# Graph network on one core: a pool that outlives the statistics, x's sums by order edges, and edge pieces that run into the second head

## The chip, the cores and the metric

The kernel runs on one core of a Trainium2 chip. The metric is the device time in microseconds (us) of one execution; three runs of the kernel before gave 1992.88, 1995.93 and 1997.72, so the median is 1995.93 us. The profile is that of one further execution, with a span of 1996.9 us. Engines are named as in the profile: PE does matmuls (PEld loads their weights), DVE is the vector engine, ACT the scalar engine, POOL is GpSimd, and SP holds the sync queue, which only issues transfers (SPq).

## The reference

Four layers run on one graph of N = 2708 nodes with F = 256 features and a dense float32 adjacency matrix `adj`. Each layer's result is added to x and normalised over the features.

```python
x = _layernorm(x + adj @ (x * W0))                     # layer 0
x = _layernorm(x + layernormed_attention(x, adj))      # layer 1, four heads
x = _layernorm(x + layer2(x, adj, adj))                # layer 2, below
x = _layernorm(x + layer3(x, adj))                     # cat(x, adj @ (x @ Wn.T) / (degree + 1)) @ Wl.T

def _gat_head(h, node_adj, edge_adj, W, a):            # layer 2, one of K = 3 heads
    hW = h @ W
    hp = (node_adj > 0) @ hW
    hm = (node_adj < 0) @ hW
    e_plus = leaky_relu(concat([hp, hm]) @ a)[:, 0]
    e_minus = leaky_relu(concat([hm, hp]) @ a)[:, 0]
    att = where(edge_adj > 0, e_plus[None, :], NEG_INF)
    att = where(edge_adj < 0, e_minus[None, :], att)
    return softmax(att, axis=1) * edge_adj @ hW

# layer 2: adj0 is adj with a zero diagonal, d its diagonal
edge_output = gru(adj0 @ h, h, edge weights)
edge_support = mean over k of _gat_head(h, adj0, adj0, gat_W[k], gat_a[k])
node_output = gru(edge_support, h, node weights)
return d * edge_output + d * node_output
```

With the inputs of this kernel no element of `adj` is negative; a separate branch, not taken here, would deal with negative ones.

## The kernel before

Rows are handled as NT = 22 tiles of P = 128 rows (the last has 20). The adjacency is read in float32, transposed in advance (`adj_t`), and every float32 matmul appears in the profile as two passes. Layers 0 and 1 run first and end near 690 us. The change concerns what follows.

**Statistics (`e_work`, lines 801 to 887).** For each of 22 rows of tiles `row_stats` (L831) needs, per head k, the maximum and the sum of exponentials over all columns. DVE makes `none` (L846), a bfloat16 row that is NEG_INF where there is no edge. Then, three times, DVE adds it to the logits `e_b` and reduces (L850), ACT takes the exponential and its sum (L855), DVE inverts the sum (L858). The rows of `adj` are loaded by gpsimd into two places, `row2` and `arow`. At the same time PE computes `adj0 @ x` for six groups of columns (`edge_sums`, L249, matmuls at L262, blocks loaded at L191 by the sync queue) and the edge GRU of the first four groups (`gru_t`, L738). The last two groups of columns (`left`, 384 and 276 wide) keep their sums in DRAM for later. Results of the statistics are transposed and stored in DRAM by `store_stats` (L781): PE transposes, ACT copies to a row tile `sr` (L790), gpsimd stores it (L796). Nine tiles, those that the first unit needs, are stored inside this stage; the other 13 tiles form four runs for later (`other_stats`, L1165).

**Attention (L1180 to L1215).** The columns are cut into two halves of NH = 1354, and each half into three units of 512, 512 and 330. Per unit u and head k a loop runs over c = 0 to 10: a step takes tiles c and c + 11 of one half together with both halves of the columns, a block of 1 MB at full width. `load_blocks` (L934) loads it and POOL zeroes the diagonal pieces (L950). The blocks go round through three places: two buffers of "blk" in the left pool, and the tail of `turn` for every third. ACT makes p from the statistics row `st_k` (L1193, L1196), DVE multiplies p by the block (L1197), and `step` (L974) forms four sums on DVE (L980 to L983) and seven matmuls (L993), which is a product of 2x2 blocks with seven instead of eight multiplications. The other operands of it are x itself and four sums per c of x's quarters, `xq[c]`, made by `quarter_sums` (L958; four DVE operations each) in the first head of the first unit and kept. The seven accumulators fill seven of PSUM's eight banks. At the end of a head `sums` (L997) copies m1 to "m1s" on ACT (L1001) and combines the accumulators on DVE (L1004 to L1011); L1213 multiplies by the inverse sums.

**Small pieces between matmuls.** PE's last PSUM bank, `bank`, serves work that is cut into pieces by Python generators. `step` calls `between()` (L1173) after its third and its sixth matmul, two slots in a step, and each slot runs one piece: first from `urgent` (the projection of the head before, L1029, four pieces), then from `later` (the edge cells of the two left groups, L1156, 16 pieces; `other_stats`, four pieces; node cells of the unit before). In the first head `later` is filled after c = 1 with edge cells and then the statistics, and at c = 10 a loop empties it before the head's sums:

```python
if u == 0 and k == 0 and c == MH - 1:
    while later:
        between()
    node_w = load_weights()
```

`sr` of `other_stats` and `m1s` of `sums` share the tag "m1s", which has one buffer.

**Layer 3 (L1240 to L1262)** uses the same `step` and `sums` on layer 2's result, with blocks loaded straight into p (`load_pairs`, L915), three units, no heads.

**What sets the order.** The kernel is written through a framework that orders each engine's instructions at compile time, by program order and a model of when inputs are ready; an instruction later in the text may so come earlier in its engine's queue. A pool of buffers lies on a stack from the left or the right end of SBUF; a pool opened after another was closed takes over its memory, and each buffer waits for the last users of the buffers that it covers. `n_left` and `n_right` of the attention take over memory of the statistics' pools. [...]

Of the kernel before, what the change touches and what calls it, by code (L numbers as in the profile page):

```python
# [19 lines left out]
P = 128  # L20
# [7 lines left out]
def kernel(  # L28
# [770 lines left out]
    for s in (fall_stack, mask_stack, m_stack, ps_t_stack):  # L799
        s.close()  # L800
    with pool("e_work") as ework:
        with (
# [28 lines left out]
            def row_stats(i):  # L831
# [12 lines left out]
                nc.vector.tensor_tensor(blk, blk, offdiag[:n, :n], ALU.mult)  # L844
                none = rows.tile([P, N], BF16, tag="none", name="none", bufs=2)
                nc.vector.tensor_scalar(none[:n], a[:n], 0.0, NEG_INF, ALU.is_equal, ALU.mult)  # L846
# [46 lines left out]
    with (  # L893
# [5 lines left out]
        ps_a = ps_stack.enter_context(pool("ps_a", 1, space=PSUM))  # L899
        node_w = lwn = None  # L900
        loaded = 0

        def bank():
            return banks.tile([P, W], F32, tag="bank", name="bank")

        def load_stats(u, k, i):

            w = units[u][1]
            dst = nleft.tile([P, 2, W], F32, tag=f"st{i}", name=f"st{i}", bufs=2 - i)
            d = st_d[u][i * K + k]  # L910
            src = bass.AP(tensor=d.tensor, offset=d.offset, ap=[[0, P], [W, 2], [1, w]])
            nc.sync.dma_start(dst[:, :, :w], src)
            return dst
# [20 lines left out]
        def load_blocks(u, c):  # L934
# [3 lines left out]
            if loaded % 3 == 2:  # L938

                s = turn[:, NT * F - 4 * w :].rearrange("p (m h w) -> p m h w", m=2, h=2)  # L940
            else:
                s = nleft.tile([P, 2, 2, W], F32, tag="blk", name="blk", bufs=2)
            loaded += 1
# [53 lines left out]
        def sums(m, w):  # L997

            m1, m26, m75, m43 = m
            m1s = nleft.tile([P, W], F32, tag="m1s", name="m1s")  # L1000
            nc.scalar.copy(m1s[:, :w], m1[:, :w])  # L1001
# [8 lines left out]
            nc.vector.tensor_tensor(yq[:, 3], yq[:, 1], m75[:, 1, :w], ALU.add)  # L1010
            nc.vector.tensor_tensor(yq[:, 1:3], yq[:, 1:3], m43[:, :, :w], ALU.add)  # L1011
            return y

        def load_weights():
            wih, whh = weights(nleft, "wih", n_wih, nc.gpsimd), weights(nleft, "whh", n_whh, nc.gpsimd)
            nonlocal lwn
            lwn = load_lwn(nleft)
            wk = nleft.tile([P, K, FC, F], F32, name="wk")
            for k in range(K):
                nc.sync.dma_start(wk[:, k], gat_w[k].rearrange("(c p) j -> p c j", p=P))  # L1020
            return wih, whh, wk

        def project(k, y, est, w):

            for h in range(2):
                for j in range(FC):
                    pw = bank()
                    for f in range(FC):
                        nc.tensor.matmul(  # L1029
                            pw[:, :w], node_w[2][:, k, f, j * P : (j + 1) * P], y[:, f, h, :w],  # L1030
                            start=(f == 0), stop=(f == FC - 1),
                        )
# [98 lines left out]
        def node(u, est):  # L1131
# [3 lines left out]
            for h in range(2):  # L1135
                lo = h * NH + a
                xt, et = nxt or load_cell(lo, w)
                yt = nleft.tile([P, FC, W], F32, tag="yt", name="yt")
                yield from cell(est[h], xt, yt, w, *node_w[:2], b_node)
                nc.vector.tensor_tensor(yt[:, :, :w], yt[:, :, :w], et[:, :, :w], ALU.add)  # L1140
# [15 lines left out]
        def edge_cells():  # L1156
            wih, whh = weights(nleft, "wih", e_wih), weights(nleft, "whh", e_whh)
            for g in left:
# [3 lines left out]
                yield from cell(sup, xt, yt, w, wih, whh, b_edge)  # L1162
                nc.gpsimd.dma_start(edge_d[g][:, :, :w], yt[:, :, :w])

        def other_stats():  # L1165
            for run in runs(order[first:]):
                store_stats(bank(), nleft.tile([P, W], F32, tag="m1s", name="sr")[: 2 * K], *run)
                yield
# [11 lines left out]
        for u, (_, w) in enumerate(units):  # L1180
            est = [nleft.tile([P, FC, W], F32, tag="est", name="est", bufs=3) for h in range(2)]
            for k in range(K):
                m = accumulators()
                for c in range(MH):
                    if u == 0 and k == 0:
                        xq.append(quarter_sums(xs, c))
                    blk = load_blocks(u, c)
                    pa = nright.tile([P, 2, 2, W], F32, tag="p", name="p", bufs=3)
                    for i in range(2):
# [6 lines left out]
                        nc.scalar.activation(p[:, :, :w], p[:, :, :w], AF.Exp, scale=-1.0)  # L1196
                        nc.vector.tensor_tensor(p[:, :, :w], p[:, :, :w], blk[:, i, :, :w], ALU.mult)  # L1197
# [44 lines left out]
        for u, (_, w) in enumerate(units):  # L1242
            m = accumulators()
            for i, c in enumerate(lead):
# [8 lines left out]
                if i == MH - 3:  # L1253
                    o8 = nleft.tile([P, 2 * W * 4 // F // 2, F], F32, tag="blk", name="o8", bufs=2)
                    for j, t in enumerate(complete(u)):
                        nc.gpsimd.dma_start(o8[: sz(t), j], y3_d[t])
                step(m, pa, h3, hq[c], c, w, i == 0, i == MH - 1, range(7) if early3 else (2, 5))
            later.append(rows3(u, sums(m, w), o8))
        ps_stack.close()
        banks = ps_stack.enter_context(pool("ps_end", 8, space=PSUM))  # L1260
        while urgent or later:
            between()  # L1262


# [260 lines left out]
```

## Time and profile before

| stretch (us) | what runs | PE busy (us) | DVE busy | ACT busy | PE clock | DMA GB/s |
|---|---|---|---|---|---|---|
| 0 to 257 | layer 0 | 247.53 | 101.47 | 25.85 | 1.00 | 165 |
| 257 to 660 | layer 1 | 386.38 | 346.25 | 175.09 | 0.97, 0.99 | 135, 78 |
| 701 to 800 | statistics | 98.35 | 97.41 | 73.01 | 1.00 | 220 |
| 800 to 900 | statistics | 98.00 | 99.93 | 76.24 | 0.98 | 221 |
| 900 to 970 | end of the statistics | 68.90 | 66.52 | 52.05 | 1.00 | 123 |
| 984 to 1076 | first head of the attention | 92.00 | 66.80 | 54.02 | 0.98 | 205 |
| 1262 to 1467 | second unit | 202.93 | 148.04 | 109.84 | 1.00 | 139 |
| 1745 to 1816 | layer 3, first unit | 70.72 | 32.52 | 12.74 | 1.00 | 104 |

The columns give the time in which an engine executes within the stretch, the share of full speed that the throttle granted to PE, and what the transfers moved. A stretch in which PE is busy throughout is bound by PE; where it is not, the chain of waits tells what it waited for. Intervals between the rows are taken up in the prediction. Two groups of the page matter besides: L850, the reduction of the statistics on DVE, with 66 instructions of 2986 ns (196.8 us), and L993, the attention's and layer 3's matmuls, with 528 + 528 + 396 instructions in its three largest groups (643.2 us).

### The profile page before, as it was taken

Reading aid. Unit: us, or ns where it says so; the run is one execution under the profiler, and the core shown is the slowest. Engines: PE = TensorE matmul, PEld = TensorE weight load, DVE = VectorE, ACT = ScalarE, POOL = GpSimd, SP = SyncE. Lnnn points to the kernel's source line nnn. Section 1 sums busy time; section 2 is a strip of 40 time slices with the busy share of each in tenths; the row PEclk is TensorE's granted clock in tenths of the full one; section 3 lists DMA queues with packets and bytes.
Section 4 is the critical chain, followed back from the end, with each engine's and each line's share of the span. In section 5 each row is a group of like instructions: output and inputs, shape, how many; then the busy total and the mean of one; then the engine's idle time right before and its main releaser. Section 6 shows DMA issues by size and latency. Waiting matters only on the chain.

```text
span 1996.9 us, 21045 instructions
## 1 busy us (share of the span) xinstructions
PE 1898.2 (95%) x7028; PEld 948.3 (47%) x7028; DVE 1455.5 (73%) x2364; ACT 852.7 (43%) x1011; POOL 354.3 (18%) x522
## 2 busy tenths in 40 slices
PE   8999999999999999999797999999999999999995
PEld 7888822222333444445453444444444555554453
DVE  4343378898897699999866688686787668745664
ACT  0100144455604277777654556455555555311000
POOL 0211210014414301120302000121110101311211
PEclk9999999999999999999898999999999999999997
DMA  8344333433101766664665466454555444643753
GB/s 283 120 166 140 135 112 131 148 112 122 41 4 50 237 222 217 231 221 144 195 201 175 121 185 173 122 159 125 150 150 131 109 118 122 173 113 86 206 156 82
DMA packets 398211, 293.96 MB, mean 147 GB/s; under 512 B 105355, under 2 KB 379435, under 8 KB 390245
## 3 DMA queue, kind: packets, MB, share of 16 engines
q1 hardware_dynamic: 381180, 237.86, 40.6%
q0 software_dynamic: 10848, 50.23, 7.2%
q10 hardware_dynamic: 6064, 4.42, 0.7%
q8 instruction: 58, 0.95, 0.2%
q14 instruction: 61, 0.49, 0.1%
HBM read 280.03 MB, written 12.40 MB: 146 GB/s over the span
## 4 chain that ended last, share of the span: by engine, by line
PE 67%; DVE 12%; DMA 8%; ACT 4%; issue 3%; POOL 3%; SPq 1%; ACTq 0%; POOLq 0%; DVEq 0%
PE m L993 30%; PE acc L199 9%; PE bank L1053 6%; PE acc L650 5%; DMA turn<-in_adj_dram 4%; DVE z L850 4%; PE s L262 4%; PE bank L1029 3%; PE den L659 3%; ACT turn L597 2%; PE bank L1104 2%; ACT turn L599 2%; DMA blk<-in_adj_t_dram 1%; DVE p L668 1%; POOL bn_rs L151 1%
## 5 line engine op out<-in xcount | busy, mean ns | idle before, releaser
L668 DVE SCALAR_TENSOR_TENSOR p<-fall_b,rise,mask 128x1024 f32<-128x1024 f32 (+1 forms) x264 | 298.7, 1153 | 39.6 <-PE den L659 23.0
L1193 ACT ACTIVATE p<-st,e_neg 128x1024 f32<-128x1024 f32 (+1 forms) x198 | 197.3, 1040 | 192.7 <-PE m L993 185.9
L993 PE MATMUL m<-p,xq 128*128 128x512 f32 (+1 forms) x528 | 245.7, 547 | 0.0
L650 PE MATMUL acc<-p,h 128*64 128x512 f32 (+2 forms) x1056 | 227.5, 559 | 5.9 <-ACT sum L682 2.7
L993 PE MATMUL m<-s,xq 128*128 128x512 f32 (+1 forms) x528 | 226.3, 545 | 0.0
L850 DVE CUSTOM_DVE_ANT_0 z<-e_b,none 128x2708 f32<-128x2708 f32 (+1 forms) x66 | 196.8, 2986 | 0.3 <-DVE e_b L820 0.2
L855 ACT ACTIVATE z<-z,st 128x2708 f32<-128x2708 f32 (+1 forms) x66 | 168.6, 2554 | 62.1 <-DVE st L850 60.2
L993 PE MATMUL m<-p,x 128*128 128x512 f32 (+1 forms) x396 | 171.2, 552 | 19.3 <-DVE p L1197 13.8
L199 PE MATMUL acc<-turn,strip 128*128 128x256 f32 (+1 forms) x836 | 187.1, 379 | 0.0
L1196 ACT ACTIVATE p<-p 128x1024 f32<-128x1024 f32 (+1 forms) x198 | 179.3, 943 | 0.3
L980 DVE TENSOR_TENSOR s<-p 128x512 f32<-128x512 f32 (+1 forms) x132 | 82.7, 627 | 125.5 <-PE m L993 106.6
L262 PE MATMUL s<-blk,x 128*128 128x512 f32 (+2 forms) x416 | 164.9, 550 | 0.7 <-ACT supt L269 0.7
L1197 DVE TENSOR_TENSOR p<-p,blk 128x1024 f32<-128x1024 f32 (+1 forms) x132 | 143.6, 1104 | 29.3 <-ACT p L1196 15.4
L199 PEld LDWEIGHTS acc<-turn,strip 128*128 128x128 f32 (+1 forms) x836 | 151.9, 185 | 23.5 <-issue 0.2
L993 PEld LDWEIGHTS m<-p,xq 128*128 128x128 f32 x528 | 99.7, 191 | 98.1 <-issue 74.4
L993 PEld LDWEIGHTS m<-s,xq 128*128 128x128 f32 x528 | 99.3, 191 | 93.6 <-issue 70.6
L650 PEld LDWEIGHTS acc<-p,h 128*64 128x64 f32 x1056 | 65.0, 137 | 150.7 <-issue 118.5
L659 PE MATMUL den<-p,h 128*32 128x512 f32 (+2 forms) x1056 | 125.9, 558 | 2.3 <-DVE p L668 1.9
L151 POOL TENSOR_TENSOR bn_rs<-bn_rs,neg_half 128x1 f32<-128x1 f32 (+1 forms) x110 | 78.4, 713 | 242.6 <-DVE bn_rs L150 239.7
L993 PEld LDWEIGHTS m<-p,x 128*128 128x128 f32 x396 | 75.3, 192 | 93.4 <-issue 59.3
L262 PEld LDWEIGHTS s<-blk,x 128*128 128x128 f32 x416 | 78.8, 193 | 76.2 <-issue 62.8
L950 POOL TENSOR_TENSOR blk<-blk,offdiag 128x128 f32<-128x128 f32 (+3 forms) x50 | 53.1, 1065 | 344.8 <-DMA blk<-in_adj_t_dram 296.7
(228 smaller groups left out, 2556.6 us busy)
## 6 DMA issues: line engine op xcount, KB each, us to landing
blk<-in_adj_t_dram SPq DMA_DIRECT2D x172, 256.0 KB, 3.5
turn<-in_adj_dram SPq DMA_DIRECT2D x22, 1354.0 KB, 5.9
strip<-in_adj_t_dram SPq DMA_DIRECT2D x19, 1408.0 KB, 6.4
blk<-in_adj_t_dram SPq DMA_DIRECT2D x88, 192.0 KB, 4.0
turn<-in_adj_t_dram SPq DMA_DIRECT2D x65, 256.0 KB, 3.8
arow<-in_adj_dram POOLq DMA_DIRECT2D x10, 1354.0 KB, 6.8
turn<-in_adj_dram POOLq DMA_DIRECT2D x10, 1354.0 KB, 7.0
blk<-in_adj_t_dram SPq DMA_DIRECT2D x103, 128.0 KB, 2.6
```

What stands on the lines that cost most here:

```text
L199: nc.tensor.matmul(acc, s[:, c, :n], rhs(c), start=(c == 0), stop=(c == NT - 1))
L262: nc.tensor.matmul(acc[f][:, :w], xs[c][:, f * P : (f + 1) * P], s[:, c - c0, :w], start=(c == 0), stop=(c == NT - 1),)
L650: nc.tensor.matmul(acc[s][i * HD : (i + 1) * HD, :ws], hs[c][:, 2 * q + i, :HD], ps[i][:, p0 : p0 + ws], **flags,)
L659: nc.tensor.matmul(den[j : j + CT, :ws], hs[c][:, 2 * q + i, HD + 1 - CT :], ps[i][:, p0 : p0 + ws], **flags,)
L668: nc.vector.scalar_tensor_tensor(p[:, :w], falls[g // 2][:, 2 * q + i, :w], rise[:, c, 2 * q + i : 2 * q + i + 1], mask[:, c, at : at + w] ...
L850: nc.vector.tensor_tensor_reduce(out=z[:n], in0=e_b[:n, k, :], in1=none[:n], scale=-1.0, scalar=HIGHEST, op0=ALU.add, op1=ALU.min, accum_o ...
L855: nc.scalar.activation(z[:n], z[:n], AF.Exp, scale=-1.0, bias=st[:n, t, 0, k : k + 1], accum_out=den[:n])
L993: nc.tensor.matmul(dst[:, :w], lt, rt, start=start, stop=stop)
L1053: nc.tensor.matmul(g[:, :w], lt, rt, start=(q == 0), stop=(q == len(terms) - 1))
L1193: nc.scalar.activation(p[:, :, :w], st_k[:, :, :w], AF.Relu, scale=-1.0, bias=e_neg[:, at, k : k + 1])
L1196: nc.scalar.activation(p[:, :, :w], p[:, :, :w], AF.Exp, scale=-1.0)
L1197: nc.vector.tensor_tensor(p[:, :, :w], p[:, :, :w], blk[:, i, :, :w], ALU.mult)
```

## The change

It has five parts. A pool `hold` on the right side is opened before the statistics and closed at the very end; the first buffers of the logits row "st0", one of the three places of the blocks (and of layer 3's `o8`) move there from the left pool, so that they need not wait for memory of the statistics. To make room, `none` has one buffer in place of two. The sums of x's quarters are no longer all free to run ahead: two are made at the start, and those for c + 2 are ordered on DVE after the product of step c. The first head's pieces are not forced out at its end: the statistics come first, the edge cells run on into the second head, the head's projection has its own weights `head_w` (loaded, with `lwn`, after c = 1), the node weights are loaded after the last edge cell, and "m1s" has two buffers. In layer 3 every DVE instruction traced inside a step is ordered after the last of the `sums` before it.

`issue_after(i)` adds no wait of its own: it only puts the instructions of the block behind `i` in the queue of `i`'s engine.

```diff
+    hold_stack = ExitStack()
+    hold = hold_stack.enter_context(pool("hold", side="right"))
     with pool("e_work") as ework:
...
-                none = rows.tile([P, N], BF16, tag="none", name="none", bufs=2)
+                none = rows.tile([P, N], BF16, tag="none", name="none")
...
-            dst = nleft.tile([P, 2, W], F32, tag=f"st{i}", name=f"st{i}", bufs=2 - i)
+            dst = (nleft if i else hold).tile([P, 2, W], F32, tag=f"st{i}", name=f"st{i}", bufs=2 - i)
...
-                s = nleft.tile([P, 2, 2, W], F32, tag="blk", name="blk", bufs=2)
+                s = (nleft if loaded % 3 else hold).tile([P, 2, 2, W], F32, tag="blk", name="blk")
...
-            m1s = nleft.tile([P, W], F32, tag="m1s", name="m1s")
+            m1s = nleft.tile([P, W], F32, tag="m1s", name="m1s", bufs=2)
...
-            nc.vector.tensor_tensor(yq[:, 1:3], yq[:, 1:3], m43[:, :, :w], ALU.add)
+            nonlocal summed
+            summed = nc.vector.tensor_tensor(yq[:, 1:3], yq[:, 1:3], m43[:, :, :w], ALU.add)
...
         def load_weights():
-            wih, whh = weights(nleft, "wih", n_wih, nc.gpsimd), weights(nleft, "whh", n_whh, nc.gpsimd)
             nonlocal lwn
...
         def edge_cells():
...
+            nonlocal node_w
+            node_w = weights(nleft, "wih", n_wih, nc.gpsimd), weights(nleft, "whh", n_whh, nc.gpsimd)
...
-                    if u == 0 and k == 0:
-                        xq.append(quarter_sums(xs, c))
+                    if u == 0 and k == 0 and c == 0:
+                        xq += [quarter_sums(xs, 0), quarter_sums(xs, 1)]
...
-                        nc.vector.tensor_tensor(p[:, :, :w], p[:, :, :w], blk[:, i, :, :w], ALU.mult)
+                        made = nc.vector.tensor_tensor(p[:, :, :w], p[:, :, :w], blk[:, i, :, :w], ALU.mult)
+                    if u == 0 and k == 0 and c + 2 < MH:
+
+                        with tc.issue_after(made.ins):
+                            xq.append(quarter_sums(xs, c + 2))
                     step(m, pa, xs, xq[c], c, w, c == 0, c == MH - 1, (2, 5))
                     if u == 0 and k == 0 and c == 1:
-                        later += [edge_cells(), other_stats()]
-                    if u == 0 and k == 0 and c == MH - 1:
-                        while later:
-                            between()
-                        node_w = load_weights()
+                        later += [other_stats(), edge_cells()]
+                        head_w = load_weights()
...
-                step(m, pa, h3, hq[c], c, w, i == 0, i == MH - 1, range(7) if early3 else (2, 5))
+                with tc.issue_after(summed.ins):
+                    step(m, pa, h3, hq[c], c, w, i == 0, i == MH - 1, range(7) if early3 else (2, 5))
```

More of the change, by code (lines that the diff above doesn't have):

```diff
@@ L899 @@
         ps_a = ps_stack.enter_context(pool("ps_a", 1, space=PSUM))
-        node_w = lwn = None
+        node_w = head_w = lwn = None
+        summed = None
         loaded = 0
@@ L1020, in load_weights @@
                 nc.sync.dma_start(wk[:, k], gat_w[k].rearrange("(c p) j -> p c j", p=P))
-            return wih, whh, wk
+            return wk
         def project(k, y, est, w):
@@ L1029, in project @@
                         nc.tensor.matmul(
-                            pw[:, :w], node_w[2][:, k, f, j * P : (j + 1) * P], y[:, f, h, :w],
+                            pw[:, :w], head_w[:, k, f, j * P : (j + 1) * P], y[:, f, h, :w],
                             start=(f == 0), stop=(f == FC - 1),
@@ L1138, in node @@
                 yt = nleft.tile([P, FC, W], F32, tag="yt", name="yt")
-                yield from cell(est[h], xt, yt, w, *node_w[:2], b_node)
+                yield from cell(est[h], xt, yt, w, *node_w, b_node)
                 nc.vector.tensor_tensor(yt[:, :, :w], yt[:, :, :w], et[:, :, :w], ALU.add)
@@ L1163, in edge_cells @@
                 nc.gpsimd.dma_start(edge_d[g][:, :, :w], yt[:, :, :w])
+            nonlocal node_w
+            node_w = weights(nleft, "wih", n_wih, nc.gpsimd), weights(nleft, "whh", n_whh, nc.gpsimd)
         def other_stats():
             for run in runs(order[first:]):
-                store_stats(bank(), nleft.tile([P, W], F32, tag="m1s", name="sr")[: 2 * K], *run)
+                store_stats(bank(), nleft.tile([P, W], F32, tag="m1s", name="sr", bufs=2)[: 2 * K], *run)
                 yield
@@ L1253 @@
                 if i == MH - 3:
-                    o8 = nleft.tile([P, 2 * W * 4 // F // 2, F], F32, tag="blk", name="o8", bufs=2)
+                    o8 = (nleft if u % 2 else hold).tile([P, 4 * W // F, F], F32, tag="blk", name="o8")
                     for j, t in enumerate(complete(u)):
                         nc.gpsimd.dma_start(o8[: sz(t), j], y3_d[t])
-                step(m, pa, h3, hq[c], c, w, i == 0, i == MH - 1, range(7) if early3 else (2, 5))
+                with tc.issue_after(summed.ins):
+                    step(m, pa, h3, hq[c], c, w, i == 0, i == MH - 1, range(7) if early3 else (2, 5))
             later.append(rows3(u, sums(m, w), o8))
@@ L1262 @@
             between()
+    hold_stack.close()
     def layer3():
```

## The prediction

> **What bounds the kernel now.** I began with the page's first part: PE is busy for 1898.2 us of 1996.9, so about 99 us without a matmul are all that a change of order can win, plus what a slow clock costs after such gaps. Busy times by stretch show where the large gaps lie. The columns are PE, PEld, DVE, ACT and POOL busy, then the granted clock, DMA share and GB/s.
>
> ```profile
> PE 1898.2 (95%) x7028; PEld 948.3 (47%) x7028; DVE 1455.5 (73%) x2364; ACT 852.7 (43%) x1011; POOL 354.3 (18%) x522
> ...
> 970.00:984.00 14.00, 0.57 (x1) 0.50 (x2) 9.00 (x36) 8.60 (x10) 7.52 (x5) 0.65 1.01 280
> 1076.00:1095.00 19.00, 5.61 (x20) 2.34 (x19) 8.09 (x10) 6.68 (x9) 4.80 (x8) 0.70 0.74 224
> 1095.00:1116.00 21.00, 21.00 (x43) 8.68 (x42) 11.05 (x12) 7.53 (x9) 0.00 (x0) 0.87 0.23 72
> 1116.00:1262.00 146.00, 146.00 (x339) 63.63 (x338) 126.06 (x152) 92.30 (x93) 13.31 (x15) 1.00 0.60 168
> ```
>
> PE stands for 13.4 us at 970 to 984 and again at 1076 to 1095 (19.00 - 5.61), each time followed by a slow clock. In 1116:1262, which holds two more ends of heads, it never stands: there PE is the bound, and an end of a head is free. The chain of waits says who ends each gap (start, us, what).
>
> ```profile
> 969.73 0.37 SPq L931
> ...
> 970.21 0.44 SPq L912
> ...
> 970.70 6.08 DMA blk<-in_adj_t_dram
> ...
> 976.94 5.00 POOL blk L950
> ...
> 981.96 1.43 DVE p L1197
> ...
> 983.43 17.30 PE m L993 x34
> ```
>
> At 970 the statistics end, and only then does the sync queue issue the first logits row (L912) and the first block: load, zeroed diagonal on POOL, product on DVE, first matmul.
>
> ```profile
> 1077.04 4.12 DMA st<-sr
> ...
> 1083.14 5.30 issue
> 1088.45 2.98 DMA st<-sr
> ...
> 1092.20 1.58 DMA st<-sr
> ...
> 1093.86 0.59 ACT m1s L1001
> ...
> 1094.50 6.67 PE m L993 x8
> ```
>
> At 1076 four stores of statistics pass one after the other through one buffer, "m1s", and m1 of the head's own sums must wait for the same buffer. The eight matmul passes at 1094.50 take 6.67 us; at full clock eight take 3.43.
>
> **What the Trainium skill says.** "TensorE: Matmul & The Clock Gate", section "What's actually happening": the array falls to half its clock after an idle window and needs some microseconds of activity to come back. The trace agrees: 0.65 and 0.70 in the gaps, passes of 0.83 us (6.67 / 8) for 0.43. "SBUF — State Buffer", section "Who interferes with whom": a DVE instruction with two inputs in SBUF contends with a GpSimd instruction that reads SBUF. It agrees too: a POOL L950 of 128x128 takes 4.99 us at 976.94, amid the stream of x's sums, and 0.45 at 973.08, when DVE is idle.
>
> **The change, part by part.**
>
> (1) Start of the attention. The row st0 and block c=0 go to a pool that shares no memory with the statistics' buffers, so their loads can be issued before 970 (the sync queue waits 65.4 us on PE L262 before this point, so it has room). DMA and POOL leave the path. What remains for c=0: "p" is still in memory that the statistics use, so ACT begins after its last exp at 966.46 and runs L1193 and L1196 twice (2.19 + 1.99 = 4.2): 970.7, or 971.4 with the two copies of supt (0.39 each) between. DVE's first product is then ready at about 969.8, the second at 972.6. PE ends its own L262 at 969.66, so it starts c=0 near 970 and, with the four s operations (0.6 each), ends it near 978.2. Block c=1 stays in the left pool and is now first in the queue at 970.1; c=0's landed 6.08 us after its first issue, so 976.2; POOL takes 0.5 to 5 us, one product 1.2. c=1's first matmul comes at 978 to 983; I take 980, since DVE no longer streams sums past POOL. Before, it came at 991.74. Gain 11.5 us, 8.7 to 13.7, slow clock included.
>
> (2) Pacing of x's sums. The work is unchanged (44 operations of 0.2 us issue, 8.8 us), 8 first and 4 after each product. A step of DVE then costs 2 x 1.15 + 4 x 0.6 + 4 x 0.2 = 5.5 us, below PE's 14 x 0.43 = 6.0. I cost it at nothing; PE's matmuls hide it. Queued behind the new order edge are only sums two steps ahead.
>
> (3) "none" with one buffer. Writer and reader are both DVE, in order, and from 870 to 960 each L846 already follows the third L850 of the row before (877.32 after 874.36). Only row 1's, at 695.16, ran ahead in a wait of DVE; it moves into the busy stretch: 1.56 us later for DVE and ACT at 966. This delays c=0, but c=1's block, landing at 976, sets PE's pace: nothing.
>
> (4) First head. Statistics come first, in the four slots of c=2 and 3; 14 of 16 pieces of the edge cells follow by c=10, and 2 pass into the second head behind the projection. With two "m1s" a store of 4.1 us has two slots (7 us) before its buffer is wanted. The forced end goes: 13.4 us idle and 21 x (1 - 0.87) = 2.7 of slow clock, 16.1. The matmuls moved cost PE the same elsewhere. Earlier wk and lwn (1.3 MB) compete with blocks near 990; from 970 to 1002 some 8 MB are wanted, 250 GB/s, where 280 to 345 were moved at 970 to 990: hidden, at most 3 us. The node weights wait on gpsimd for the last edge matmul, long before the first node cell.
>
> (5) Layer 3's order edge: sums before the steps of the next unit. At its entry this helps:
>
> ```profile
> 1734.23 0.69 DVE L980 TENSOR_TENSOR s<-p 128x512 f32<-128x512 f32 x1 [7.52 <-DMA p<-in_adj_t_dram]
> ...
> 1736.17 0.83 DVE L1004 TENSOR_TENSOR yk<-m1s,m 128x660 f32<-128x660 f32 x1
> ...
> 1737.06 2.08 PE L993 MATMUL m<-p,turn 128*128 128x512 f32 x2 [4.70 <-DVE yk L1004]
> ```
>
> DVE's s of the next step waits 7.52 us for a load, and the sums L1004, ready at about 1731.6, stand behind it, and PE behind them. With sums first PE waits for the load alone (to 1735.5): 1.5 to 2.5 us, I take 2. At the two later ends of units it costs: there the s operations ran ahead, while PE was busy:
>
> ```profile
> 1850.55 0.69 DVE L980 TENSOR_TENSOR s<-p 128x512 f32<-128x512 f32 x1 [3.42 <-DMA p<-in_adj_t_dram]
> ...
> 1853.90 1.22 DVE L1004 TENSOR_TENSOR yk<-m1s,m 128x1024 f32<-128x1024 f32 x1 [0.60 <-PE m L993]
> ```
>
> Now the four sums (1.22, 1.22, 0.68, 1.22: 4.3 us) come first, then L980; its s1 is wanted by PE at 1857.2 and ready at 1858.7: 1.6 us. At 1921.93 the same sum gives 1926.7 against 1924.6: 2.1. Net 2 - 3.7 = -1.7, call it -1.5; -4 if steps behind stall too, +2 if PE's slack of 1.9 us at 1926 to 1944 absorbs the last.
>
> Sum: 11.5 + 16.1 - 1.5 = 26.1, so 1995.93 - 26 = **1970 us**.
>
> **Rivals.** (a) The stall moves by one step: c=1's block and c=2's last piece stay bound to the end of the statistics (the sync queue stood 17.5 us in c=2's load until PE ended), POOL is starved for 6.64 us as at 991.24, and c=1 starts only at 988. Part 1 is then worth 4 us, and if DMA takes 3 more: 1995.9 - 4 - 16.1 + 1.5 + 3 = 1981. For it: DMA share 1.01 at the start. Against it: c=0's 1 MB is no longer in that rush. (b) Nothing new binds, c=1 is there at 978, head 1 stays full and the entry of layer 3 gains 3 without loss at the later ends: 1995.9 - 13.7 - 16.1 - 3 = 1963. (c) Slower: a new order on all queues. If each of nine paced steps waits 2 us for its sums or for POOL (18), layer 3's edges hold each unit 4 us (8), stores of statistics queue on POOL behind L950's wait for blocks (such waits total 296.7 us) and stop PE for 6 in the single bank, and part 1 yields 4 while 16.1 stays: 1995.9 + 18 + 8 + 6 - 20 = 2008. Against it: DVE's 5.5 against PE's 6.0 per step.
>
> **How the numbers follow.** Forecast 1970: 0.60; (a) 0.20; (b) 0.09; (c) 0.06; a mixture near no change 0.05. Adding the ends of (1) and (5) gives 1964 to 1976 for the forecast, with 3 us of DMA 1979; the range reaches from (b)'s edge to beyond (a): 1961 to 1984. Faster 0.89 (forecast, a, b), same 0.05, slower 0.06.
>
> **What would show it.** Right: the first L993 within 3 us of the last L262, c=1 within 10 us after; granted clock 0.9 or more there; no PE gap over 2 us at the end of the first head; L1053 pieces after the first L1029; at layer 3's entry L1004 ahead of L980. Wrong: POOL L950 or a load of "blk" ahead of PE in the first four steps; ACT sr waiting for a store; DVE running out of work at L963 to L966; PE idle over 3 us after the sums at the later ends of units.

## The result and the profile after

The changed kernel takes 1969.89 us (median of four runs, 1969.51 to 1970.69), against 1996.51 us for the kernel before in the same set (1992.88 to 1997.72). The ratio is 0.987, with a 95% interval of 0.9853 to 0.9887: 26.6 us less. The forecast was 1970. That it was met so closely is partly luck: two of its terms were off in opposite directions.

Line numbers move by two or three: L993 is now L996, L950 is L953, L931 is L934, L912 is L915, L1193, L1196 and L1197 are L1198, L1201 and L1202, L980 is L983, L1001 and L1004 are L1004 and L1007, L1029 is L1032 and L1053 is L1056.

The first part of the page: PE does the same 7028 matmuls in 3 us less, which goes with the mean granted clock of the two executions, 0.981 before and 0.988 now; the rest of the gain is idle time.

```profile
PE 1895.1 (96%) x7028; PEld 945.7 (48%) x7028; DVE 1454.0 (74%) x2364; ACT 852.0 (43%) x1011; POOL 348.8 (18%) x522
```

The same stretches as before, with the same columns (PE, PEld, DVE, ACT and POOL busy, granted clock, DMA share, GB/s):

```profile
970.00:984.00 14.00, 13.24 (x25) 5.24 (x25) 13.97 (x29) 13.04 (x14) 6.76 (x4) 0.79 1.06 302
1076.00:1095.00 19.00, 19.00 (x51) 9.50 (x50) 11.16 (x18) 10.54 (x13) 2.59 (x4) 1.00 0.61 174
1095.00:1116.00 21.00, 21.00 (x50) 9.31 (x49) 17.55 (x21) 12.73 (x13) 1.99 (x3) 1.00 0.89 266
1116.00:1262.00 146.00, 146.00 (x339) 63.63 (x338) 119.66 (x145) 85.76 (x88) 16.65 (x18) 1.00 0.60 165
```

At 970 to 984 PE was busy for 0.57 us and is now busy for 13.24. At 1076 to 1095 it was 5.61 and is 19.00, with no slow stretch behind it. A fixed stretch of time holds other work in the two kernels, so these rows show that both gaps are gone, not what that was worth.

**The start of the attention**, PE in order of time:

```profile
964.29 2.02 PE L262 MATMUL s<-turn,x 128*128 128x276 f32 x8
...
968.70 1.77 PE L996 MATMUL m<-p,x 128*128 128x512 f32 x2 [1.94 <-DVE p L1202]
971.11 2.08 PE L996 MATMUL m<-p,x 128*128 128x512 f32 x2 [0.64 <-DVE p L1202]
...
978.96 1.88 PE L996 MATMUL m<-p,x 128*128 128x512 f32 x4
```

The last L262 ends at 966.31 and the first L996 starts 2.4 us later, where it was 13.8. Step c = 1 begins at 978.96. The chain of waits shows what sets that (start, us, what):

```profile
965.06 1.04 ACT p L1198
...
968.68 1.07 ACT p L1201
...
970.97 0.29 DVE xq L966
...
973.55 0.60 DVE s L983
974.15 0.20 DVE xq L969
974.35 0.61 DVE p L984
...
975.01 5.40 PE m L996 x11
```

No transfer and no POOL piece is left in it. ACT makes p, DVE multiplies, then a run of x's first sums (L966 to L969, 970.97 to 973.55) goes ahead of the s operations, and PE is held until one of those, L984, is done.

**To compare many executions** the table below uses offsets that don't depend on what ran earlier: microseconds from the start of the last L262 matmul to the first L993 or L996, to the copy of m1 on ACT that ends heads 1, 2 and 9, then the length of layer 3's last unit (from its second such copy to its third), and the end of the span. The two rows of the changed kernel show how far they can be trusted: they differ by 1.2 at head 1, by 1.1 at head 2, by 0.9 at head 9, and by 0.1 in the last unit.

| kernel | first matmul | head 1 | head 2 | head 9 | last unit | end |
|---|---|---|---|---|---|---|
| before | 14.2 | 124.6 | 196.8 | 758.9 | 49.0 | 1027.7 |
| changed | 2.8 | 91.6 | 169.7 | 731.8 | 51.0 | 1001.8 |
| changed, again (e12) | 2.8 | 92.8 | 170.9 | 732.8 | 50.9 | 1001.5 |
| e1 pool alone | 2.8 | 115.1 | 186.7 | 748.5 | 48.8 | 1016.6 |
| e2 first head alone | 15.5 | 100.8 | 178.7 | 740.5 | 48.7 | 1006.8 |
| e3 no pacing | 2.8 | 91.9 | 170.0 | 731.7 | 50.8 | 1000.4 |
| e4 no edge in layer 3 | 2.8 | 91.4 | 169.4 | 731.2 | 48.8 | 999.6 |
| e5 before, two m1s | 14.8 | 118.7 | 190.1 | 752.2 | 48.7 | 1018.8 |
| e6 changed, forced end | 2.8 | 91.2 | 169.5 | 731.7 | 51.0 | 999.3 |
| e7 changed, one m1s | 2.8 | 93.1 | 171.1 | 733.4 | 51.0 | 1003.4 |
| e8 changed, row left | 14.4 | 99.4 | 177.5 | 739.5 | 51.0 | 1007.4 |
| e9 before, lists exchanged | 16.0 | 102.2 | 180.3 | 742.3 | 48.7 | 1008.9 |
| e10 changed, block left | 9.7 | 96.5 | 174.6 | 736.7 | 51.1 | 1007.1 |
| e11 edge at one unit | 2.8 | 92.3 | 170.4 | 732.3 | 48.8 | 1000.3 |

Head 1 alone is no fair measure between kernels that move pieces of work into head 2; head 2 is. From there to head 9 all take about 562 us (562.1 before, 562.1 changed), so what is won by head 2 is kept: 27.1 us. Layer 3 gives back part.

### The profile page after: what moved, and what is told of

Same layout as the page of the kernel before. It is cut to its first block, busy times and chain, and to the rows that moved or that the text cites. A ratio compares the mean times of both kernels' runs of the same rounds, so it can differ in the third digit from the quotient of the medians.

```text
span 1967.7 us, 21033 instructions
## 1 busy us (share of the span) xinstructions
PE 1895.1 (96%) x7028; PEld 945.7 (48%) x7028; DVE 1454.0 (74%) x2364; ACT 852.0 (43%) x1011; POOL 348.8 (18%) x522
## 4 chain that ended last, share of the span: by engine, by line
PE 70%; DVE 17%; issue 5%; DMA 3%; POOL 2%; ACT 1%; SPq 1%; ACTq 0%; DVEq 0%; POOLq 0%
PE m L996 31%; PE acc L650 9%; PE acc L199 9%; DVE z L852 8%; PE bank L1056 6%; PE den L659 5%; PE bank L1032 3%; PE bank L1107 2%; DVE p L668 2%; DVE none L848 1%; POOL bn_rs L151 1%; PE acc L423 1%; PE pm L338 1%; DMA p<-in_adj_t_dram 1%; SPq L934 1%
## 5 line engine op out<-in xcount | busy, mean ns | idle before, releaser
L1198 ACT ACTIVATE p<-st,e_neg 128x1024 f32<-128x1024 f32 (+1 forms) x198 | 197.5, 1040 | 186.1 <-PE m L996 183.6
L996 PE MATMUL m<-p,xq 128*128 128x512 f32 (+1 forms) x528 | 245.6, 547 | 0.8 <-DVE p L984 0.6
L996 PE MATMUL m<-s,xq 128*128 128x512 f32 (+1 forms) x528 | 224.7, 542 | 0.4 <-DVE s L985 0.4
L1201 ACT ACTIVATE p<-p 128x1024 f32<-128x1024 f32 (+1 forms) x198 | 179.5, 943 | 0.3
L996 PE MATMUL m<-p,x 128*128 128x512 f32 (+1 forms) x396 | 169.5, 547 | 2.6 <-DVE p L1202 2.6
L1202 DVE TENSOR_TENSOR p<-p,blk 128x1024 f32<-128x1024 f32 (+1 forms) x132 | 142.6, 1095 | 30.9 <-ACT p L1201 16.3
L262 PE MATMUL s<-blk,x 128*128 128x512 f32 (+2 forms) x416 | 162.9, 545 | 0.0
L983 DVE TENSOR_TENSOR s<-p 128x512 f32<-128x512 f32 (+1 forms) x132 | 82.8, 628 | 97.9 <-PE m L996 83.8
L996 PEld LDWEIGHTS m<-p,xq 128*128 128x128 f32 x528 | 99.3, 191 | 99.6 <-issue 74.6
L996 PEld LDWEIGHTS m<-s,xq 128*128 128x128 f32 x528 | 98.7, 190 | 93.6 <-issue 70.3
L262 PEld LDWEIGHTS s<-blk,x 128*128 128x128 f32 x416 | 77.9, 190 | 74.2 <-issue 62.5
L996 PEld LDWEIGHTS m<-p,x 128*128 128x128 f32 x396 | 74.6, 191 | 76.7 <-issue 59.1
L165 ACT COPY xt<-tr 128x256 f32<-128x256 f32 (+1 forms) x44 | 16.0, 363 | 209.2 <-PE tr L163 203.5
```

What stands on the lines that cost most here:

```text
L262: nc.tensor.matmul(acc[f][:, :w], xs[c][:, f * P : (f + 1) * P], s[:, c - c0, :w], start=(c == 0), stop=(c == NT - 1),)
L996: nc.tensor.matmul(dst[:, :w], lt, rt, start=start, stop=stop)
L1198: nc.scalar.activation(p[:, :, :w], st_k[:, :, :w], AF.Relu, scale=-1.0, bias=e_neg[:, at, k : k + 1])
L1202: made = nc.vector.tensor_tensor(p[:, :, :w], p[:, :, :w], blk[:, i, :, :w], ALU.mult)
```

## The experiments

Each ratio is to the kernel before, run on the same chip as the experiment, with a 95% interval. In the first set (e1 to e4) the kernel before took 1999.47 us, in the second (e5 to e8) 1996.58, in the third (e9 to e12) 1996.88.

### e1 and e2: one part alone

e1 is the kernel before with the pool `hold` (first row, one block place, `o8`) and the single `none`:

```diff
+    hold = hold_stack.enter_context(pool("hold", side="right"))
...
-                none = rows.tile([P, N], BF16, tag="none", name="none", bufs=2)
+                none = rows.tile([P, N], BF16, tag="none", name="none")
...
-            dst = nleft.tile([P, 2, W], F32, tag=f"st{i}", name=f"st{i}", bufs=2 - i)
+            dst = (nleft if i else hold).tile([P, 2, W], F32, tag=f"st{i}", name=f"st{i}", bufs=2 - i)
...
-                s = nleft.tile([P, 2, 2, W], F32, tag="blk", name="blk", bufs=2)
+                s = (nleft if loaded % 3 else hold).tile([P, 2, 2, W], F32, tag="blk", name="blk")
...
```

> The kernel before with the pool alone (first logits row, one block place, one buffer of none); sums of x not paced, first head forced out at its end, no order edge in layer 3. Theory A (two separate gains, the pool worth about 10 us by itself): 1986 us (1983 to 1988), c=0's first matmul within 4 us of the last L262, the gap at the end of the first head still 13 us. Rival B (the pool is worth something only together with the pacing, since a stream of 44 sums stands on DVE ahead of c=0's product and starves POOL): 1992 to 1997, first matmul 8 us or more after the last L262.

e2 is the kernel before with the first head's part: statistics first, no forced end, `head_w`, node weights after the edge cells, two "m1s":

```diff
...
-                        later += [edge_cells(), other_stats()]
-                    if u == 0 and k == 0 and c == MH - 1:
-                        while later:
-                            between()
-                        node_w = load_weights()
+                        later += [other_stats(), edge_cells()]
+                        head_w = load_weights()
```

> The kernel before with the first head's part alone (statistics first, edge cells run on, weights split, two m1s); no pool, no pacing, no order edge in layer 3. Theory A: the end of the first head gives 16 to 18 us by itself, 1979 us (1977 to 1981), no PE gap over 2 us at that end, the gap of 13 us at the start of the attention unchanged. Rival C (part of that gap is paid back, because statistics and weights now compete with the first blocks): 1983 to 1988.

Measured: e1 1987.40 us, ratio 0.9943 (0.9925 to 0.9961); e2 1976.17 us, ratio 0.9885 (0.9866 to 0.9905). e1's time is in the range that was expected; e2's is 0.8 us below its own. At head 2 the pool alone wins 10.1 us and the first head's part alone 18.1; together 27.1. Each leaves the other's gap: the end of the first head in e1, and the start in e2, in the columns used above:

```profile
1064.00:1082.50 18.50, 5.67 (x22) 2.23 (x20) 8.29 (x10) 6.10 (x9) 5.33 (x9) 0.76 0.78 238
```

```profile
966.70:981.80 15.10, 2.11 (x14) 0.64 (x11) 8.46 (x36) 6.64 (x9) 6.43 (x8) 0.68 1.00 279
```

The 2.11 us in e2's row are nearly all the 13 transposes of the statistics left for the first head: with the statistics first in the list, they fill a part of the start gap. In the changed kernel that gap is gone and most of them run later, among the matmuls. That could be why the two gains together are 1 us less than their sum, but 1 us is no more than two executions of one kernel differ by, so it isn't shown.

### e3 and e4: without the pacing, without layer 3's edge

```diff
-                        xq += [quarter_sums(xs, 0), quarter_sums(xs, 1)]
+                        xq.append(quarter_sums(xs, c))
...
-                        with tc.issue_after(made.ins):
-                            xq.append(quarter_sums(xs, c + 2))
```

> The changed kernel with x's sums free to run ahead again; all else changed. Theory A (pacing hides under PE and is worth little): 1970 to 1973. Rival B (without it the stream of sums stands ahead of the first products and the pool's gain is lost): 1976 to 1981, first matmul of the attention 8 us or more after the last L262, POOL L953 stretched to 5 us or more.

```diff
-                with tc.issue_after(summed.ins):
-                    step(m, pa, h3, hq[c], c, w, i == 0, i == MH - 1, range(7) if early3 else (2, 5))
+                step(m, pa, h3, hq[c], c, w, i == 0, i == MH - 1, range(7) if early3 else (2, 5))
```

> The changed kernel without the order edge in layer 3; all else changed. Theory A (the edge gains about 1.2 at the entry and loses 2 to 3 at the later ends of units): 1968.5 us (1967 to 1970), sums behind the first s operations at the entry again. Rival D (the edge is what keeps layer 3 from losing more): 1972 to 1976.

Measured: e3 1970.30 us, ratio 0.9861 (0.9839 to 0.9882); e4 1972.38 us, ratio 0.9864 (0.9847 to 0.988). Neither can be told from the changed kernel by its time. e4's time is above the 1967 to 1970 that were expected and in the rival's range, but the kernel before was also slower in this set, by 3 us, than beside the first runs of the changed kernel, and e4's ratio is that of the changed kernel. In the offsets e3 is the same up to head 9: the pacing is worth nothing here. Without the edge, the last unit of layer 3 is 2.2 us shorter (48.8 for 51.0), as in every kernel without it, which speaks against the rival.

### e5, e6, e7 and e9: what closed the gap at the end of the first head?

The part has three ingredients: statistics ahead of the edge cells, a second buffer for "m1s" and "sr", and no forced end. e5 adds only the buffer to the kernel before:

```diff
-            m1s = nleft.tile([P, W], F32, tag="m1s", name="m1s")
+            m1s = nleft.tile([P, W], F32, tag="m1s", name="m1s", bufs=2)
...
-                store_stats(bank(), nleft.tile([P, W], F32, tag="m1s", name="sr")[: 2 * K], *run)
+                store_stats(bank(), nleft.tile([P, W], F32, tag="m1s", name="sr", bufs=2)[: 2 * K], *run)
```

> The kernel before with one edit: m1s and sr take turns in two buffers in place of one; edge cells still come first, statistics last, and the loop at c = 10 still empties the list. Theory 'order': the four stores of statistics are still run one close behind the other at the end of the head, so two buffers only let them overlap in pairs: about half of the 13.4 us idle stays, the first head ends 116 to 119 us after the last L262 pass (before: 124.6), total about 6 to 8 us less, ratio 0.996 to 0.997. Rival 'buffer': the single buffer was the whole cause: first head ends near 107, ratio 0.991. Third: another wait (the single bank, the DMA queue) ends the gap as late as before: 124, ratio 1.000.

Measured: 1989.34 us, ratio 0.9969 (0.9955 to 0.9983), 6.7 us at head 2. About half of the gap stays, and the chain of waits of e5 says why:

```profile
1077.75 0.47 ACT sr L790
...
1079.70 0.01 POOLq L796
1079.71 5.50 DMA st<-sr
...
1085.24 0.59 ACT m1s L1001
```

The last store takes 5.50 us to land, and m1's copy needs a buffer that a store still reads: two buffers shorten the queue of stores at the head's end, but don't remove it.

e6 puts the forced end back into the changed kernel, and e7 takes the second buffer out of it:

```diff
+                    if u == 0 and k == 0 and c == MH - 1:
+                        while later:
+                            between()
```

> The changed kernel with the loop at c = 10 back: what is left of the list (two edge pieces of 16) is forced out ahead of the head's sums; statistics still come first and m1s has two buffers. Theory 'order': with the stores long done, forcing two pieces costs one or two waits of PE for ACT and DVE in a cell, 0 to 5 us at the end of the first head (mark 91.6 to 97 us) and less at the end of the second; ratio to the kernel before 0.987 to 0.989. Rival 'forcing': the forced end itself was the cost, so most of 16 us comes back: second head ends at 182 or later in place of 169.7, ratio 0.994 or more.

```diff
-            m1s = nleft.tile([P, W], F32, tag="m1s", name="m1s", bufs=2)
+            m1s = nleft.tile([P, W], F32, tag="m1s", name="m1s")
...
-                store_stats(bank(), nleft.tile([P, W], F32, tag="m1s", name="sr", bufs=2)[: 2 * K], *run)
+                store_stats(bank(), nleft.tile([P, W], F32, tag="m1s", name="sr")[: 2 * K], *run)
```

> The changed kernel with one buffer for m1s and sr, all else as changed. Theory 'order': the four stores run in four slots some 3.5 us apart at c = 2 and 3, each takes about 4 us, so PE's single bank may wait for ACT's copy 1 to 3 us in all, partly hidden by other matmuls; the end of the head is not touched: ratio 0.987 to 0.988, first head ends 91.6 to 94. Rival 'buffer': second buffer is needed: the first head ends 98 or later, ratio 0.991 or more.

Measured: e6 1972.79 us, ratio 0.9882 (0.9865 to 0.9898); e7 1974.57 us, ratio 0.9881 (0.9859 to 0.9902). At head 2 they stand at 169.5 and 171.1, and the two executions of the changed kernel at 169.7 and 170.9. Neither the forced end nor the missing buffer costs anything that stands out from that difference, once the statistics come first.

e9 is the test from the other side, two words exchanged in the kernel before, with its single buffer and its forced end:

```diff
-                        later += [edge_cells(), other_stats()]
+                        later += [other_stats(), edge_cells()]
```

> The kernel before with two words exchanged: in the first head the four runs of statistics come first in the list and the edge cells second; one buffer for m1s and sr, and the loop at c = 10, stay. Theory 'order': this alone gives what the run-on part gave (18.2 us at the end of the second head): the first head shows no PE gap over 2 us at its end and the second head ends 178 to 181 us after the last L262 pass (before 196.8); ratio 0.990 to 0.992. Rival 'two buffers and run-on are needed': with one buffer, or with the edge pieces forced out, a gap of 5 us or more stays at the end of the first head, second head at 184 to 192, ratio 0.994 to 0.998.

Measured: 1978.02 us, ratio 0.9902 (0.9887 to 0.9918). PE's row at the end of e9's first head:

```profile
1060.00:1092.00 32.00, 32.00 (x92) 17.08 (x91) 26.85 (x37) 18.99 (x25) 5.07 (x8) 1.00 0.56 176
```

The gap is gone. Head 2 ends at 180.3, 16.5 us before that of the kernel before, though e9's own start is 2 us later (16.0 for 14.2). So the order of the two lists is the cause: the stores are the last work in the kernel before, and in e9 the last of them is issued at 1011.0, some 58 us before the head's end. The other two ingredients add at most the 1.6 us by which e2 is ahead of e9 at head 2, of which e9's later start (0.5 us later than e2's) is a part.

### e8 and e10: the row or the block?

e8 moves the first row back to the left pool in the changed kernel, e10 the blocks' third place (and `o8` with it):

```diff
-            dst = (nleft if i else hold).tile([P, 2, W], F32, tag=f"st{i}", name=f"st{i}", bufs=2 - i)
+            dst = nleft.tile([P, 2, W], F32, tag=f"st{i}", name=f"st{i}", bufs=2 - i)
```

> The changed kernel with the first logits row st0 back in the left pool; the first block stays in the new pool. Theory 'both are needed': the row's load waits for the end of the statistics, is issued near the last L262 and lands 2 to 5 us later, then ACT's p (4.2 us) and DVE's product: the first L996 comes 9 to 12 us after the last L262 pass began (after: 2.8, before: 14.1), and the first head ends 3 to 7 us later than 91.6, because c = 1's block alone would let c = 1 start at +13. Rival 'the block is all': the row is small, first L996 within 5 us, mark 91.6 to 92.5. Rival 'row is all': first head ends 10 us later.

```diff
-                s = (nleft if loaded % 3 else hold).tile([P, 2, 2, W], F32, tag="blk", name="blk")
+                s = nleft.tile([P, 2, 2, W], F32, tag="blk", name="blk", bufs=2)
...
```

> The changed kernel with the blocks' third place and o8 back in the left pool (two buffers there); the logits row st0 stays in the new pool. Theory 'both are needed': c = 0's load is issued only after the last L262, lands 6 us later, then POOL (0.5 to 5 us) and DVE (1.2): first L996 at +9 to +14 (after: +2.8), first head ends 97 to 100 (after: 91.6); ratio to before 0.990 to 0.991. Rival 'row is what counts', since with the row late the whole gap came back: first L996 within +6, first head within 2 us of 91.6.

Measured: e8 1976.17 us, ratio 0.991 (0.9885 to 0.9935); e10 1973.59 us, ratio 0.9887 (0.987 to 0.9904). The block behaves nearly as expected: its first matmul comes at 9.7, in the range; head 1, at 96.5, and the ratio are a little better than the ranges. Its chain of waits is that of the kernel before, shorter by POOL's delay:

```profile
968.39 4.62 DMA blk<-in_adj_t_dram
...
973.09 0.42 POOL blk L953
...
973.53 1.24 DVE p L1202
...
974.81 19.97 PE m L996 x40
```

The row was a surprise: its first matmul came at 14.4, later than the 9 to 12 that were expected, head 1 ended 7.8 us later where 3 to 7 were expected, and the whole start gap is back although the block had long landed. ACT in order of time, in e8:

```profile
966.40 0.57 ACT L790 COPY sr<-bank 6x512 f32<-6x512 f32 x1 [0.67 <-PE bank L787]
967.67 0.57 ACT L790 COPY sr<-bank 6x512 f32<-6x512 f32 x1 [0.69 <-PE bank L787]
974.61 0.36 ACT L790 COPY sr<-bank 6x256 f32<-6x256 f32 x1 [6.37 <-DMA st<-sr]
974.88 2.18 ACT L1198 ACTIVATE p<-st,e_neg 128x1024 f32<-128x1024 f32 x2
```

In e8 three copies of statistics stand ahead of p on ACT; in the changed kernel the first of them comes at 977.59, behind the p of three steps. The likely reason is that p can't start with the end of the statistics here, and the compile-time order filled the place. The third copy needs a buffer that a store still reads, and waits 6.37 us for it; p, DVE's product and PE stand behind. The chain of waits shows that the store was itself issued late, after a POOL piece of another block:

```profile
968.46 0.45 POOL turn L953
...
968.95 5.56 DMA st<-sr
```

A small row that is late cost the full gap through what was put in its place. At head 2 the row back in the left pool costs 7.8 us (6.7 against the second execution), the block 4.9 (3.8), and both together, changed against e2, 9.0 (7.8). Put the other way round, of these 9.0 us the row alone in the new pool gives 4.1 (e10) and the block alone 1.2 (e8).

### e11 and e12: the edge only where it helps, and the changed kernel again

```diff
-                with tc.issue_after(summed.ins):
+                with tc.issue_after(summed.ins) if u == 0 else ExitStack():
```

> The changed kernel with layer 3's order edge kept at its first unit alone, where PE waits for a load, and dropped at the two later ends. Theory: entry and first unit as in the changed kernel (120 to 121 us from the end of the ninth head), last unit 48.8 to 49 in place of 51.0, so 2 to 2.5 us less in all: ratio to the changed kernel 0.9988, to before 0.9855 to 0.9865. Rival: without the edge the order of the last units changes elsewhere too and the total stays within 1 us.

> The changed kernel itself beside the other three on one chip: ratio to before 0.986 to 0.988, first L996 at +2.8, first head ends at 91.6, second at 169.7, last unit of layer 3 takes 51 us.

Measured: e11 1966.94 us, ratio 0.9848 (0.9835 to 0.9862); e12 1970.62 us, ratio 0.9876 (0.9859 to 0.9894). The two intervals just touch, but each of e11's five runs (1963.35 to 1967.84) is below each of the four of the changed kernel beside it (1969.75 to 1975.60), so e11 is most likely faster, by somewhat more than the 2 to 2.5 us that were expected. The last unit is shown: 48.8 us for 51.0. DVE at the end of the second unit, first in the changed kernel:

```profile
1890.59 1.22 DVE L1007 TENSOR_TENSOR yk<-m1s,m 128x1024 f32<-128x1024 f32 x1 [7.62 <-PE m L996]
1891.84 1.22 DVE L1010 TENSOR_TENSOR yk<-yk,m 128x1024 f32<-128x1024 f32 x1
1893.10 0.69 DVE L1013 TENSOR_TENSOR yk<-yk,m 128x512 f32<-128x512 f32 x1
1893.89 1.22 DVE L1015 TENSOR_TENSOR yk<-yk,m 128x1024 f32<-128x1024 f32 x1
1895.03 0.50 DVE L983 TENSOR_TENSOR s<-p 128x330 f32<-128x330 f32 x1
```

and then in e11:

```profile
1885.56 0.50 DVE L983 TENSOR_TENSOR s<-p 128x330 f32<-128x330 f32 x1 [3.26 <-PE m L996]
...
1889.92 1.22 DVE L1007 TENSOR_TENSOR yk<-m1s,m 128x1024 f32<-128x1024 f32 x1 [2.37 <-PE m L996]
```

With the edge DVE stands idle for 7.62 us ahead of the sums while the next unit's s could be made; without it they are made in that time.

## Why the prediction was right or wrong

**Start, forecast 11.5 (8.7 to 13.7).** It gave 10.1 alone (e1) and 9.0 on top of the other part (changed against e2; 7.8 with e12), so below the value each time, and with e12 below the lower bound too. Loads and POOL left the path as forecast. Counted from the end of the last L262, c = 0 was to end 8.5 us later and c = 1 to start, bound by its block, at 10.3. In the changed kernel both came at 12.65; before, c = 1 started at 22.1. The block wasn't the bound: POOL was done with it at 975.83, and DVE, busy with c = 0 until then, took it at 976.30. Two terms that the prediction put at nothing came onto the path, and a third came beside them.

The first is in (3): the 1.56 us by which DVE and ACT fall behind with one `none` was costed at nothing because c = 1's block would set PE's pace. The delayed piece is seen in the traces: the second `none` was made at 695.16 before, ahead of the first reductions, and is made at 710.56 now, after three of them. ACT's last instruction of the statistics ended 3.2 us ahead of PE's last L262 in the four executions with two buffers of `none` (before, e2, e5, e9) and 1.3 ahead in all ten with one, so about 2 us came onto the path. The new pool or a part of it goes with the single buffer in all ten, so the two are parted only by the code: nothing else that the statistics run was edited.

The second is in (2): x's first sums were called hidden by matmuls. In the first step there are no matmuls to hide them; they stand for 2.6 us (970.97 to 973.55) between the product and the s operations. This is the pacing's doing in part: in e3, without it, three of these sums stand there in place of eleven, and L984 ends 7.0 us after the last L262 in place of 8.6. Yet c = 1 starts no earlier in e3 (13.1).

The third is **the granted clock**. Of the signs named for this part, the first matmul came in time (2.4 us after the last L262, within 3), c = 1 hardly missed it (10.3 us after the first, within 10), but the clock, which was to be 0.9 or more, was 0.67 from 968.70 to 979.00, after a gap of only 2.4 us. In e3 it was 0.50 from 971 to 977, though the last of the s operations was done at 975.07:

```profile
971.00:977.00 6.00, 5.56 (x7) 2.33 (x8) 6.00 (x20) 6.00 (x8) 3.23 (x2) 0.50 1.09 347
```

So sums and clock hold c = 0 back side by side, and taking away the sums alone won nothing. The clock also explains why executions differ. In all six executions with pool and pacing in full, L984 ends 8.6 us after the last L262, and eight passes of c = 0 are left. In e4 (first two lines) they take 3.54 us, at full clock from 977.0 on; in e12 (last two) 5.24, at 0.67; in the changed kernel 3.95.

```profile
976.68 1.12 PE L996 MATMUL m<-p,xq 128*128 128x512 f32 x2 [0.39 <-DVE p L984]
...
980.22 1.88 PE L996 MATMUL m<-p,x 128*128 128x512 f32 x4
...
976.93 1.59 PE L996 MATMUL m<-p,xq 128*128 128x512 f32 x2 [1.50 <-DVE p L984]
...
982.17 1.88 PE L996 MATMUL m<-p,x 128*128 128x512 f32 x4
```

c = 1 starts 12.2 us after the last L262 in e4, 12.65 in the changed kernel and 13.9 in e12. The 1.3 us between the last two account for the 1.2 between their rows at head 1. In the sum, c = 0 ended 4.1 us later than forecast: 1.8 with the late second product, 0.4 with the clock in the last eight passes, and the other 1.9 in between, with the sums. The forecast had left 1.8 between its end and c = 1, so 2.3 remain.

**First head's end, forecast 16.1.** It gave 18.1 alone (e2) and, beside the new pool, 17.0 (27.1 - 10.1). The idle time and the slow clock behind it vanished as forecast. Where the 1 to 2 us more come from isn't shown; the transposes that fill the start gap in e2 can be a part of it there. The step on its cause was half right: statistics first is what does it (16.5 with the order alone, e9). "The forced end goes" and the two buffers, to which the text gave the gain as well, are worth nothing beyond it that can be seen (e6, e7).

**Pacing, forecast 0.** Right in the number (e3), but not for the reason given: in the first step the paced sums do delay DVE's L984, by 1.6 us, and in e3, without it, the slow clock took its place.

**Layer 3's edge, forecast a loss of 1.5 (+2 at the entry, then -1.6 and -2.1).** The last unit lost 2.2, near the 2.1 worked out, though not in one wait of PE for s1: PE's longest wait there is 0.98 us, and where the rest went isn't shown. At the end before it the loss was 0.3 (68.35 us for 68.03 without, e4 and e11), not 1.6. The gain at the entry isn't shown: from head 9 to the first unit's end the eight executions with the edge there took 118.8 to 121.4 us (mean 120.3) and the six without it 120.0 to 122.2 (mean 120.9). PE does now wait for the load alone, as forecast:

```profile
1704.79 1.13 PE L996 MATMUL m<-p,turn 128*128 128x512 f32 x2 [2.04 <-DMA p<-in_adj_t_dram]
...
1708.90 1.29 PE L996 MATMUL m<-p,turn 128*128 128x512 f32 x2 [2.13 <-DMA p<-in_adj_t_dram]
```

From head 9 to the end of the program the seven executions with the edge at every unit take 269.0 us on average (267.6 to 270.4) and the six without it 267.5 (266.3 to 268.7). So the net is a loss of about 1.5, as on record, but with both the gain at the entry and the first loss smaller than forecast.

**The rivals.** The stall did not move by one step (a): PE is busy for all of 979.00 to 997.30. (b) asked for a start worth 13.7 and an entry worth 3; neither came. Of (c) nothing was seen in the first steps or at the ends of units. Some sums of the prediction are off by about 1 us, without effect on this: (a) comes to 1980, not 1981, and the upper ends 1976 and 1979 to 1975 and 1978.

The sum 11.5 + 16.1 - 1.5 = 26.1 met the 26.6 of the runs because the start's shortfall of 1.4 to 2.5 was made up by 1 to 2 us at the first head's end. That these two cancel was luck.

## What to carry to other kernels

Where a stall ends in a transfer that waits for a buffer, look first at where the work that fills the buffer stands in its list: work whose results must land goes first and work that only fills time last; here two words won 16.5 us where a second buffer alone won 6.7. To free a first load from old memory, free everything that its first consumer needs: a small input that stayed behind brought the whole gap back here, with other work in its place in the order made at compile time. And at the start of a stage little is hidden: cost each operation between the first product and the first matmul in full, even those that cost nothing in every later step, and beside them a slow clock after even a short gap.

## What the runs showed of the hardware

Two things were not expected. The first is how much the time of one small POOL operation varies. The second line shows two operations L953 that took 7.60 us together, 7.33 of it one of 128x128 elements, amid DVE's products and sums; PE didn't wait for them. In the first line one of the same size took 0.45:

```profile
971.53 0.45 POOL L953 TENSOR_TENSOR blk<-blk,offdiag 128x128 f32<-128x128 f32 x1 [1.65 <-DMA blk<-in_adj_t_dram]
...
979.74 7.60 POOL L953 TENSOR_TENSOR blk<-blk,offdiag 128x128 f32<-128x128 f32 x2 [0.76 <-DMA blk<-in_adj_t_dram]
```

A busy DVE isn't enough to explain it, though the prediction read it so from one pair: DVE was in the middle of x's sums at 971.53 too (970.97 to 973.55), and in e12 the operation that took 7.33 here took 0.50, also beside a busy DVE. In the first 30 us after the last L262, over all the traces, L950 or L953 on 128x128 took 0.41 to 0.47 us while DVE was idle, and 0.40 to 10.39 while DVE was busy for most of it. What decides between short and long there stays open.

The second is the clock after a short gap. After 2.4 us with only four small transposes in it, the changed kernel had a clock of 0.51 from 969 to 971 in one execution. In another (e12) it was 1.00 until 977 and then 0.57 until 981, and c = 1 came 1.3 us later there.
